# Two-layer kernel: the decay scans of the second layer write into the tile they read, and that tile gets two buffers

## The chip, the cores and the metric

One NeuronCore of a Trainium2 chip runs the whole program. The metric is device time in microseconds (us) of one launch. The engines are TensorE (PE; its weight loads are listed as PEld), VectorE (DVE), ScalarE (ACT), GpSimd (POOL) and SyncE (SP), which issues nearly all DMAs.

## The reference

The input is `x` of shape (16, 512, 128): 16 batches of 512 tokens. Two layers follow each other.

```python
xn = _layernorm(x)
x  = x + L0_attn(xn) + L0_ffn(xn)      # selective-scan mixer; 8 experts, top 1
xn = _layernorm(x)
x  = x + L1_attn(xn) + L1_ffn(xn)      # the layer that this change is in
```

The second layer's mixer is a causal linear attention with 16 heads, a decay for each head and token, and a factor `lam_ts` that is picked by the "level" of the pair of tokens (how high the highest bit is in which their positions differ):

```python
g  = A * softplus(x @ Wdt.T + dt_bias)         # per token and head
cg = cumsum(g, axis=1)
decay = exp(cg[t] - cg[s]) for s <= t, else 0
Wmat  = scores * decay * lam_ts                # scores = Q K^T / 8
Y = einsum('bhts,bshd->bthd', Wmat, V)
out = layernorm(Y @ Wout.T + x) * ln_g + ln_b
```

The second layer's other branch is a small gated recurrence over the 16 batches with a projection at its end.

## The kernel before, in words

**Two phases.** The loop `for i in range(-2, NB + 3)` runs layer one, a batch (a *block*) of 512 tokens at a time, in overlapping stages. The loop `for b in range(NB + 1)` runs the mixer of layer two over the same 16 blocks. In the profiled execution layer one takes the first 300 us and layer two the rest, some 31 us a block. Results of layer one go through HBM (`d_xf`, `d_xh`, `d_xl`, `d_xt`, `d_x1`).

**Second layer, block b.** The 512 tokens are split into chunks of `C` = 32.
- `load1(b)` and `gates(b)` load the block and make the projections (`pp`) and the step sizes; `g3` is the log decay, split into three bf16 parts.
- `factors(b)` turns `g3` into chunk decays (`pe`, then `ex`), makes the level factors `la`, and transposes the level and decay rows (`pld`). Through HBM (`dde`) the decay rows are spread over partitions into the tile **`dd`** by four DMAs (L1102 to L1104); the level rows go through `dld` into `R`.
- `products(b)`: 16 heads, three 512-wide matmuls each into a bank `pT`, copied by ACT into `th_all`.
- `states(b)`: chunk states `pG` into `Gs`, with the tiles `bv`, `t`, `tiles`.
- `diagonal(b)`: four scans on DVE make the decays inside a chunk: each reads a quarter of `dd` and writes a quarter of the tile **`dec`** (L1212 to L1218). Then four multiplications by the level factors, out of the banks `pl`.
- `diagonal2(b)`: four multiplications of `dec` by the scores, out of the banks `pS`; then 64 small matmuls (128 recorded) read `dec` into the bank `pyd`, which is added to `ysum`.
- `upper(b)`, `upper2(b)`: the part between chunks (`pU`, `yq`, `pY`, `aY`), added to `ysum` on POOL, for the last block on DVE.
- `finish(b)`: `pyt` (transpose of `ysum`), `yT`, the output projection `po1` (shown as `b_po`), the sum `o` with the block, layer norm (`lc_st`, `lc_mv`, `lc_r`, `lc_nb`, four activations on `o`, a multiplication on POOL, an addition on DVE) and the store.

**Buffers.** `bt(shape, dtype, tag, name)` takes a tile from a pool by tag. A tag has one buffer unless `BUFS` says otherwise (L503). `dec` and `dd` have one each, 8 KB in a partition. So the scans of block b+1 wait until the 128 `pyd` matmuls of block b have read `dec`, and the DMAs that fill `dd` for block b+1 wait until the scans of block b have read it.

**Lending.** Layer one borrows the second layer's tiles (`lend`, L594 to L622): the split input `xnh`/`xnl` of its projections lies in the buffer of `dec`, the scratch tiles `th`, `xt`, `bx` in the buffer of `dd`.

**Who sets the order.** Every instruction is first recorded by the class `Plan`; `flush()` then simulates all engines with assumed durations and picks, engine by engine, the order in which the instructions are emitted. Each engine then runs its list in that order, and an instruction that waits holds all behind it on the same engine. A sort key takes an operation's due time, the length of what depends on it, a weight by the engine and the name of the written tile, and a small pseudo-random term with a fixed seed:

```python
kind = o.eng[0] + ":" + kind.tensor.name.rstrip("0123456789_")
o.key -= 1000.0 * (URGENT.get(kind, 0.0) + STAGES.get(stage(...), {}).get(kind, 0.0))
o.key += rng.uniform(-JIT, JIT)
```

`URGENT` (L50) has the entry `"v:lent_dec_xnh": -0.5`, for DVE instructions that write the lent tile of that name. All recorded instructions are emitted from one line, L479, so the profile's groups are told apart by tile names.

Of the kernel before, what the change touches and what calls it, by code (L numbers as in the profile page):

```python
# [12 lines left out]
F32 = mybir.dt.float32  # L13
F32R = mybir.dt.float32r
# [9 lines left out]
P = 128  # L24
NG = 4
NH = 16
EPS = 1e-5
C = 32
# [464 lines left out]
def two_layer_kernel(ctx: ExitStack, tc: tile.TileContext, a: dict, out: bass.AP):  # L493
# [6 lines left out]
    sp = ctx.enter_context(tc.tile_pool(name="s", bufs=1))  # L500
    ps = ctx.enter_context(tc.tile_pool(name="ps", bufs=1, space=PSUM))
    dram = ctx.enter_context(tc.tile_pool(name="dram", bufs=1, space=DRAM))
    BUFS = {k: 2 for k in ("xf", "xh", "xl", "vz", "aY", "bv", "vbd")}  # L503
    BUFS.update({"xt": 3, "hh": 3})

    PA, PB = 5000.0, 5000.0

    def bank(name, tag="tr", shape=(P, 512), dt=F32):
        return nc.bank(ps, shape, dt, tag, name)

    def bt(shape, dt, tag, name, bufs=None):
        return nc.tile(sp, shape, dt, tag, name, bufs or BUFS.get(tag, 1))

# [80 lines left out]
    def lend(tag, k, dt, users, cols=T):  # L594
        t = bt([P, k, cols], dt, tag, "lent_" + tag + "_" + (users[0] if users else "w"))
        for i, u in enumerate(users):
            ring.setdefault(u, []).append(t[:, i, :])
        return t
# [4 lines left out]
    wbig = lend("vbd", 4, F32R, []).rearrange("p (s k) c -> p s (k c)", s=2)  # L603
    wbig = wbig[:, 0, :], wbig[:, 1, :]
    lend("vbd", 4, F32, ["x1", "x1", "xn1", "hs"])
    lend("dec", 4, F32R, ["xnh", "xnh", "xnl", "xnl"])


    Gs = wt([P, NH, 17, 8], F32, "Gs")
# [83 lines left out]
    for e in range(8):  # L693
        j = e % 4
# [271 lines left out]
    vbd = []  # L966

    def namer1(b):
        return lambda s: f"b_{s}_{b}"
# [237 lines left out]
    def diagonal(b):  # L1207

        n, d = namer1(b), B[b]
        R = d["R"]  # L1210

        dec = bt([P, NH, NG, C], F32, "dec", n("dec"))  # L1212
        for q in range(4):
            hs = slice(4 * q, 4 * q + 4)
            nc.vector.tensor_tensor_scan(
                dec[:, hs].rearrange("p h j t -> p (h j t)"), d["dd"][:, hs].rearrange("p h t -> p (h t)"),
                upat.rearrange("p q t -> p (q t)"), 0.0, op0=ALU.mult, op1=ALU.add,
            )  # L1218
        Rt = R.rearrange("r h (t j) -> r t h j", j=NG)
        for q in range(4):  # L1220
            pl = bank(n(f"pl{q}"))
            for i in range(8):
                t = 8 * q + i
                nc.tensor.matmul(
                    pl[:, i * 64 : (i + 1) * 64], sell[:, t, :], Rt[:, t], start=True, stop=True
                )
            dv = dec[:, :, :, 8 * q : 8 * q + 8].rearrange("p h j t -> p j h t")
            nc.vector.tensor_tensor(
                dv, dv, pl.rearrange("p (t h j) -> p j h t", h=NH, j=NG), op=ALU.mult
            )  # L1230
        d["dec"] = dec
# [62 lines left out]
    for i in range(-2, NB + 3):  # L1294
# [49 lines left out]
        if i == NB + 1:  # L1344
            states(0)
            diagonal(0)
            products(0, "pj", range(8, NH))
# [15 lines left out]
    for b in range(NB + 1):  # L1363
        nc.base = (NB + 4) * PA + (b + 1) * PB
        nc.start_group(LNEXP)
        if 0 < b < NB:
            states(b)
        if b + 2 < NB:
            load1(b + 2)
        if b + 1 < NB:  # L1370
            gates(b + 1)
        if b:
            finish(b - 1)
        if b < NB:
            if b:
                diagonal(b)
            for q in range(4):
                if b:
                    products(b, heads=range(4 * q, 4 * q + 4))
                if q:  # L1380
                    upper(b, q - 1)
        if b + 1 < NB:
            factors(b + 1)
        if b < NB:
            upper(b, 3)
            upper2(b)
            diagonal2(b)
        if b + 1 < NB:
            nc.start_group(EXPTANH)
            cell_out(b + 1)  # L1390
# [113 lines left out]
```

## Time and profile before

| | |
|---|---|
| median of 3 runs | 829.51 us (827.62 to 831.28) |
| the profiled execution's own time | 828.71 us |
| its span, first to last instruction | 826.5 us |
| busy, share of the span | PE 96%, DVE 89%, ACT 76%, POOL 25% |
| `dec` and `dd`: instructions of layer two | 64 scans, 128 multiplications, 64 DMAs into `dd` |

The span is 2.2 us shorter than the execution's own time; that difference lies around the instructions. Matmuls are pipelined and their ends are modelled, so a PE that is busy all the time is not one at its peak. What idle PE time there is, and what ended it, is read from the list of waits and from the timeline.

### The profile page before, as it was taken

What the parts mean: (1) busy time and instruction counts of PE and PEld (TensorE: products, weight loads), DVE (VectorE), ACT (ScalarE), POOL (GpSimd) and SP (SyncE); (2) the same over time, 40 slices, a digit from 0 to 9 for tenths busy, and PEclk for the clock granted to TensorE, in tenths of its full rate; (3) what the DMA queues carried; (4) which work ended last, traced back from release to release, by engine and by line L of the source; (5) the groups of instructions that cost most, each with busy time, mean ns of one, the idle gap of its engine ahead of it and who ended that gap; (6) DMA issues with size and microseconds to landing.
All of it is one profiled execution on the core that took longest, in us unless ns stands there. A gap on an engine that the chain in (4) does not pass through costs nothing.

```text
span 826.5 us, 27744 instructions
## 1 busy us (share of the span) xinstructions
PE 790.8 (96%) x11432; PEld 605.4 (73%) x11432; DVE 735.5 (89%) x1889; ACT 631.9 (76%) x1322; POOL 206.7 (25%) x236
## 2 busy tenths in 40 slices
PE   7899999999999998999999999999999999999994
PEld 4577878777888776787677778768677778677772
DVE  5799999999998996798989999888999989899885
ACT  6788898989898887876696697587588577587573
POOL 2200000000000110333343343533433523433521
PEclk9799999999999998999999999999999999999998
DMA  9516444334333334254345346435346426536311
GB/s 226 132 52 205 141 154 127 103 113 136 112 109 108 109 115 139 78 135 117 104 128 147 96 130 150 130 94 151 100 123 158 136 79 156 130 87 157 88 52 40
DMA packets 92402, 100.18 MB, mean 121 GB/s; under 512 B 26532, under 2 KB 63788, under 8 KB 90156
## 3 DMA queue, kind: packets, MB, share of 16 engines
q1 hardware_dynamic: 92276, 98.41, 42.5%
q8 instruction: 90, 1.47, 0.7%
q14 instruction: 36, 0.29, 0.1%
HBM read 63.70 MB, written 34.67 MB: 119 GB/s over the span
## 4 chain that ended last, share of the span: by engine, by line
PE 56%; DVE 18%; ACT 15%; DMA 4%; issue 3%; POOL 3%; SPq 0%; ACTq 0%; DVEq 0%; POOLq 0%
PE b_pT L479 11%; PE pg L479 6%; DVE b_dec L479 5%; ACT th_all L479 5%; PE b_pU L479 5%; PE po L479 5%; PE pm L479 4%; PE b_pY L479 3%; PE b_pS L479 2%; DVE b_la L479 2%; PE pC L479 2%; ACT L479 2%; PE pxi L479 2%; PE pz L479 2%; PE b_pp L479 2%
## 5 line engine op out<-in xcount | busy, mean ns | idle before, releaser
L479 ACT COPY th_all<-b_pT 128x512 f32<-128x512 f32 x256 | 145.0, 622 | 25.9 <-PE b_pT L479 20.0
L479 PE MATMUL b_pT<-b_xh,A_h 128*128 128x512 f32 x256 | 108.1, 422 | 1.2 <-DVE b_tiles L479 0.9
L479 POOL TENSOR_TENSOR b_u<-b_u,b_vz 128x704 f32<-128x704 f32 x16 | 27.9, 1743 | 298.7 <-DVE b_vz L479 256.9
L479 PE MATMUL b_pT<-b_xh,A_l 128*128 128x512 f32 x256 | 100.8, 394 | 0.0
L479 PE MATMUL b_pT<-b_xl,A_h 128*128 128x512 f32 x256 | 100.4, 392 | 0.0
L479 ACT ACT_TABLE_LOAD x71 | 91.1, 1283 | 1.9 <-PEq L1494 0.7
L479 DVE TENSOR_TENSOR_SCAN b_dec<-b_dd,upat 128x512 f32<-128x512 f32 x64 | 77.8, 1226 | 4.5 <-PE b_pyd L479 3.0
L479 PEld LDWEIGHTS b_pU<-th_all,Gs 128*32 128x32 f32 x4096 | 61.3, 110 | 19.2 <-issue 9.0
L479 PE MATMUL b_pU<-th_all,Gs 128*32 128x64 f32 x4096 | 70.9, 220 | 2.1 <-ACT th_all L479 0.9
L479 PE MATMUL b_pS<-th_all,b_xf 128*32 128x512 f32 x512 | 60.3, 594 | 0.4 <-ACT th_all L479 0.4
L479 PEld LDWEIGHTS b_pT<-b_xh,A_h 128*128 128x128 f32 x256 | 48.1, 188 | 15.3 <-PE b_pT L479 1.3
L479 PEld LDWEIGHTS b_pT<-b_xh,A_l 128*128 128x128 f32 x256 | 48.1, 188 | 10.9
L479 PEld LDWEIGHTS b_pT<-b_xl,A_h 128*128 128x128 f32 x256 | 48.3, 189 | 6.9
L479 ACT COPY b_yq<-b_pU 128x512 f32<-128x512 f32 x64 | 38.5, 614 | 13.8 <-PE b_pU L479 13.4
L479 DVE TENSOR_TENSOR b_dec<-b_dec,b_pl 128x512 f32<-128x512 f32 x64 | 40.3, 680 | 9.4 <-PE b_pl L479 9.4
L479 DVE TENSOR_TENSOR b_dec<-b_pS,b_dec 128x512 f32<-128x512 f32 x64 | 43.6, 681 | 1.2 <-PE b_pS L479 1.0
L479 DVE TENSOR_TENSOR b_la<-b_ex,b_sp 64x32 f32<-64x32 f32 (+3 forms) x160 | 41.4, 284 | 1.7
L479 ACT ACTIVATE lent_vbd_x<-lent_vbd_x,lb_nb,lb_r 128x128 f32<-128x128 f32 x64 | 29.6, 489 | 11.8 <-DVE lb_nb L479 8.7
L479 DVE TENSOR_TENSOR b_aY<-b_pY,b_la 128x384 f32<-128x384 f32 (+1 forms) x64 | 33.9, 543 | 4.4 <-POOL b_ysum L479 3.0
L479 PE MATMUL pg<-lent_yq_x1h,lent_hh_w 128*128 128x512 f32 x96 | 33.8, 431 | 1.1 <-DVE lent_yq_x1h L479 1.1
L479 PE MATMUL pm<-Gs,ww 128*128 128x512 f32 x64 | 34.5, 621 | 0.0
L479 ACT ACTIVATE b_o<-b_o,b_lc_nb,b_lc_r 128x128 f32<-128x128 f32 x64 | 33.7, 552 | 0.9 <-DVE b_lc_nb L479 0.9
(268 smaller groups left out, 2154.7 us busy)
## 6 DMA issues: line engine op xcount, KB each, us to landing
b_dd<-b_dde SPq DMA_DIRECT2D x64, 256.0 KB, 5.7
b_dld<-b_ld SPq DMA_DIRECT2D x48, 96.0 KB, 2.8
b_R<-b_dld SPq DMA_DIRECT2D x16, 288.0 KB
d_x<-lent_vbd_x SPq DMA_DIRECT2D x16, 256.0 KB, 3.4
d_xt<-lent_vbd_x SPq DMA_DIRECT2D x16, 256.0 KB, 3.7
b_xt<-d_xt SPq DMA_DIRECT2D x16, 256.0 KB, 3.7
d_xf<-th_all SPq DMA_DIRECT2D x16, 256.0 KB, 2.0
d_xh<-lent_yq_x1h SPq DMA_DIRECT2D x16, 256.0 KB, 3.6
```

Of the source, the lines that this page charges most:

```text
L479: o.inst = getattr(getattr(self.nc, o.eng), o.name)(*o.args, **o.kw)
```

## The change

The scans of block b write over `dd` itself, and everything that read or wrote `dec` afterwards goes on that tile (`dec` is now a view of it). The tag `dec` is gone and `dd` has two buffers, so the memory is the same. Layer one's `xnh`/`xnl` are lent one buffer of `dd`, and its `th`, `xt`, `bx` the other. The DMAs for block b+1 now wait for the last reader of block b-1 (`pyd`), and the scans of block b+1 wait for their DMA alone.

```diff
-    BUFS = {k: 2 for k in ("xf", "xh", "xl", "vz", "aY", "bv", "vbd")}
+    BUFS = {k: 2 for k in ("xf", "xh", "xl", "vz", "aY", "bv", "vbd", "dd")}
...
-    lend("dec", 4, F32R, ["xnh", "xnh", "xnl", "xnl"])
+    lend("dd", 4, F32R, ["xnh", "xnh", "xnl", "xnl"])
...
-        dec = bt([P, NH, NG, C], F32, "dec", n("dec"))
+        dec = d["dd"].rearrange("p h (j t) -> p h j t", j=NG)
         for q in range(4):
             hs = slice(4 * q, 4 * q + 4)
             nc.vector.tensor_tensor_scan(
-                dec[:, hs].rearrange("p h j t -> p (h j t)"), d["dd"][:, hs].rearrange("p h t -> p (h t)"),
+                d["dd"][:, hs].rearrange("p h t -> p (h t)"), d["dd"][:, hs].rearrange("p h t -> p (h t)"),
                 upat.rearrange("p q t -> p (q t)"), 0.0, op0=ALU.mult, op1=ALU.add,
             )
```

No instruction is added or removed. The lent tile that was `lent_dec_xnh` is now named `lent_dd_xnh`, and what was `b_dec` is `b_dd`; the entry `"v:lent_dec_xnh"` of `URGENT` no longer matches a tile.

## The prediction

> **What bounds the kernel now.** I read the page first, then PE's own waits, the instructions on `dec`, the stretches of the second layer and the timeline of the last block, and last the two instruction orders, engine by engine.
>
> ```profile
> PE 790.8 (96%) x11432; PEld 605.4 (73%) x11432; DVE 735.5 (89%) x1889; ACT 631.9 (76%) x1322; POOL 206.7 (25%) x236
> ...
> L479 DVE TENSOR_TENSOR_SCAN b_dec<-b_dd,upat 128x512 f32<-128x512 f32 x64 | 77.8, 1226 | 4.5 <-PE b_pyd L479 3.0
> ```
>
> PE is the bound. The scans cost DVE 77.8 us, and DVE stood idle ahead of them for 4.5 us: 3.0 us until `pyd` had read `dec`, and 1.3 us for a DMA into `dd`, by the answer on the tile. These are the two waits that the change loosens. What reaches PE is in PE's own waits:
>
> ```profile
> PE b_pe L479 <- DVE b_g L479: 4.4, 6, 1.6
> ...
> PE b_pyd L479 <- DVE b_dec L479: 0.9, 1, 0.9
> ```
>
> The columns are us in total, times, longest. PE waited for `dec` once, 0.9 us, and that at 812 us, in the last block. Its largest DVE wait is for the log decays `g3` (shown as `b_g`) ahead of `pe`. In 18 stretches of 25 us from 350 to 800 us, PE is busy 439.2 of 450 us: 10.8 us idle in all. That is the most that a better order of the middle can give back; `pyd` returns every 29.9 us (605.54, 635.59, 665.44) at best and every 30.9 us on average (389.26 to 759.88, 12 blocks), which says the same: some 12 us.
>
> The end is different:
>
> ```profile
> 800.00:825.00 25.00, 14.24 (x412) 9.87 (x404) 15.92 (x45) 9.03 (x21) 3.82 (x3) 0.87 0.17 47
> ```
>
> After the start of the slice the columns are PE, PEld, DVE, ACT, POOL, the granted clock and the DMAs. Here no engine is full: a chain through all of them sets the end, and each step on it costs its own time.
>
> **The change part by part.** Counts stay: 64 scans at 1226 ns, 128 multiplications at 680 ns, 64 DMAs. A scan that writes where it reads is not in this trace; the nearest rows are the multiplications, which already write over `b_dec`, at 680 and 681 ns, like other two-input operations of their size (684 ns for the split of `xnh`). I take 1226 ns unchanged; the reach is -0.1 to +0.1 us a scan, no more than 6 us on DVE and nearly none on PE in the middle.
>
> `dd`'s DMAs now wait for `pyd` of two blocks before instead of the last block's scans. Both are past when the DMAs issue at a block's end, so nothing behind them on SP's queue is held longer: 0. Layer one's orders of PE, DVE and ACT are the same until its last block, so the lost weight `"v:lent_dec_xnh"` moves nothing there; on SP two constant loads near 18 us, `sell` and `upat`, swap, and `upat` is wanted first at 314 us: 0.
>
> What remains is the order of layer two, which `Plan` makes anew. Three things in it have a price.
>
> *The middle, DVE.* The scans now stand ahead of `pyd`. Before, `pyd` of the last block mostly stood behind the products of head 6; now it stands behind head 8 to head 15, and `ysum`, `pyt`, `po1` and the layer norm follow it into the second half of the block. The waits of 3.0 and 1.3 us go. They were on DVE and PE waited for `dec` only at the end, so I count 0 on PE; the bounds are 0 and -4.3 us. The first DVE wait to come after them is the 9.4 us for `pl`, which PE itself sets.
>
> The Trainium skill (Trainium Kernel Development and Optimization, Best Practices) advises two buffers so that DMA overlaps compute. By that rule the second `dd` buffer would be a gain; the trace shows the load hidden but for 1.3 us.
>
> *The middle, PE.* In blocks 9, 10 and 13 the new order is `pyd`, two `pl` banks, then `pyt`, which needs `ysum`. From the end of `pyd` to `pyt` takes 0.96 us (813.38 to 814.34 in the last block: 0.22 us, the 0.68 us addition, 0.06 us); two `pl` banks fill 0.41 us. So 0.55 us of new PE wait, three times: +1.7 us. Against it, changes between whole-array products and products on a part of it fall from 219 to 214, at some 0.1 us each (a `pT` matmul follows another after 0.23 us, but after 0.31 to 0.34 us on either side of `pyd`): -0.5 us.
>
> *The end.* In the old order `po1` of block 13 and `pyd` of block 14 stood ahead of head 3 of the last block's products; in the new one they come after head 15, between the third and the fourth `pl`. So the layer norms of blocks 13 and 14, which ran beside the last products, now fall into the tail. I count from the first `pl` of block 15 (796.70 us), which comes 1.09 + 1.31 = 2.4 us earlier since those two are gone from ahead of it:
> - PE: three `pl` 0.8, `po1` 1.1, `pyd` 1.3, `pl` 0.4, first `pS` 0.9: at 4.5 us.
> - DVE: multiplication, `Gs`, `ysum` of block 14 and the norm statistics of block 13 among them, 2.7 us with latency: at 7.4 us.
> - ACT: latency and two `lc_r` 0.7, table load 1.28, `hh` 0.5, four activations on `o` 1.65, table load 1.28, four `yq` with `yT` between at 0.5 each: at 15.4 us. Before, the products' copies covered these.
> - PE: last `pY` 0.6, `po1` of block 14 1.1, last `pS` 0.9: at 18.0 us.
> - DVE: other work to 18.6, the last multiplication 0.6, then five `ysum` 1.0, `aY3` 0.6, the statistics of block 14 1.2: at 22.0 us.
> - ACT: `lc_r` 0.6, load 1.28, four activations 1.65, `yT` of block 15 0.5: at 26.1 us. `po1` of block 15 1.2, and DVE's last `o` starts at 27.4 us.
>
> Before, that `o` started at 816.86 us, 20.2 us from the same mark. So +27.4 - 20.2 - 2.4 = +4.8 us. These lines show the old tail, where the four activations were over 4.7 us before `yT` wanted ACT:
>
> ```profile
> 807.31 1.28 ACT L479 ACT_TABLE_LOAD   x1
> 808.61 1.65 ACT L479 ACTIVATE b_o<-b_o,b_lc_nb,b_lc_r 128x128 f32<-128x128 f32 x4
> 815.03 0.58 ACT L479 COPY b_yT<-b_pyt 128x512 f32<-128x512 f32 x1 [4.77 <-PE b_pyt L479]
> ```
>
> After the load of 1.28 us the next activation starts within 0.02 us, so I price a load at 1.28. The Trainium skill (ScalarE: Activation LUTs, What ACT_TABLE_LOAD costs) gives about 1283 ns for the load and about 1380 ns of drain on top. By that rule the three loads of the new tail would add 3 x 1.38 = 4.1 us, an estimate from that page, which speaks further against the change; the trace has no such gap.
>
> The tail's sum is good to about 4 us either way: work that I laid end to end may overlap, or waits that I left out may come.
>
> **Sum.** 4.8 + 1.7 - 0.5 = +6.0 us. On the profiled execution's 828.7 us that is 834.7; on the median, which is 0.8 us higher, 835.5. I say 835. The likeliest case's own range is 831 to 840.
>
> **The rivals.**
> - *Faster.* The free scans let DVE reach `g3` earlier, so that PE's waits of 4.4 us for `g3`, 1.0 us for `pld` and most of the 4.3 us go: -8 us; and the tail overlaps, +2 instead of +4.8. With +1.2 for the rest (1.7 - 0.5) that is 829.5 - 4.8 = 824.7; for 822 the middle must give nearly all its 10.8 us. For it: the waits exist and DVE is 89% busy. Against it: in the new order the `g3` chain still lies between the multiplications by `pS`. It decides if the tail costs under 2 us.
> - *No difference.* The tail costs 4.8 us and the middle gives back as much: 829 to 832. For it: the middle is planned anew in every block, with 10.8 us of waits to draw from. Against it: nothing in the new order takes the `g3` wait away.
> - *Worse in the middle.* With the layer norms pushed to where DVE multiplies by `pl` and `pS`, the `g3` chain comes later and PE waits another 0.7 us in each of 13 blocks: 835 + 9 = 844. For it: in blocks 5 and 12 statistics of the norm stand among those multiplications. It decides if the waits of `pe` for `g3` pass 10 us.
> - *It doesn't do what it says.* If an in-place scan were slower than 1226 ns, by more than 0.3 us each, DVE would gain 1.2 us a block and pass PE: above 844.
>
> **How the numbers follow.** The measurement tells about 0.5%, 4.15 us, from no change: 825.4 and 833.7 are the limits. My forecast's case has 0.50, worse in the middle 0.20, a slow in-place scan 0.02, no difference 0.15, faster 0.13. Of the forecast's case about a twelfth, 0.04, ends under 833.7 and belongs to "same". So faster 0.13, same 0.19, slower 0.68. The range reaches down to 826 (which leaves out about 0.13) and up to 845 (about 0.07 above).
>
> **What would show it.** Right: the first `pl` of block 15 comes earlier against the end of the span, the tail from there grows from 29.8 us to 34 to 39 us; the four activations on `o` of block 14 stand between the last statistics and the last `yT`; DVE's waits for `pyd` at the scans are gone, 1226 ns stays; PE waits for `ysum` ahead of `pyt` near 0.55 us in blocks 9, 10 and 13. Wrong: a tail of about 30 us; `g3` waits far from 4.4 us; scans of another length; a start of layer two that moves.

## The result, and the profile after

The changed kernel takes 842.26 us (median of 4 runs, 841.59 to 844.64), the kernel before in the same comparison 829.50 us. The ratio is 1.0159 [1.0129, 1.0189]: 12.8 us slower. The profiled execution took 842.17 us, its span 840.4 us, 13.9 us more than before.

First the page, with the engines' busy time and the group of the scans:

```profile
span 840.4 us, 27755 instructions
...
PE 794.6 (95%) x11432; PEld 610.2 (73%) x11432; DVE 729.9 (87%) x1889; ACT 633.7 (75%) x1322; POOL 206.5 (25%) x236
...
L479 DVE TENSOR_TENSOR_SCAN b_dd<-b_dd,upat 128x512 f32<-128x512 f32 x64 | 75.5, 1209 | 1.5 <-DMA b_dd<-b_dde 1.3
```

The change does on DVE what it says: an in-place scan takes 1209 ns instead of 1226, and the idle time ahead of the scans falls from 4.5 to 1.5 us, with no wait for `pyd` left. No count changed. PE is busy 3.8 us longer and the span is 13.9 us longer, so some 10 us of the loss are PE time in which nothing ran.

The mark of the prediction, the first `pl` of block 15, splits it. Here is the mark before, and then, of the kernel after, the first and the last instructions of PE's timeline behind it, and DVE's last sum `o`:

```profile
796.70 0.88 PE L479 MATMUL b_pl<-b_R,sell 72*128 72x64 bf16 x24
```

```profile
802.40 0.88 PE L479 MATMUL b_pl<-b_R,sell 72*128 72x64 bf16 x24
803.12 1.14 PE L479 MATMUL b_po<-pkl,b_yT 128*128 128x128 f32 x8
804.19 1.30 PE L479 MATMUL b_pyd<-b_vbd,b_dd 128*32 128x32 f32 x128
...
828.97 2.08 PE L479 MATMUL b_po<-pkl,b_yT 128*128 128x128 f32 x8 [1.91 <-ACT b_yT L479]
```

```profile
831.08 0.69 DVE L479 TENSOR_TENSOR b_o<-b_po,b_xt 128x512 f32<-128x512 f32 x1 [0.56 <-PE b_po L479]
```

| | before | after | difference | with the 2.4 us of `po1` and `pyd` that moved past the mark |
|---|---|---|---|---|
| span's start to the mark | 796.70 | 802.40 | +5.7 | **+8.1** (forecast +1.2) |
| mark to the span's end | 29.8 | 38.0 | +8.2 | **+5.8** (forecast +4.8) |

The tail came nearly as forecast. The stretch ahead of it did not. PE's own waits of the after kernel from 350 to 800 us (us in total, times, longest) show what stands there now:

```profile
PE b_pY L479 <- ACT b_yq L479: 2.6, 1, 2.6
PE b_pU L479 <- DVE Gs L479: 2.3, 4, 0.8
PE b_pU L479 <- issue: 1.9, 2, 1.4
PE b_pe L479 <- DVE b_g L479: 1.8, 4, 0.8
PE b_pl L479 <- issue: 1.8, 1, 1.8
PE b_pyt L479 <- POOL b_o L479: 1.7, 1, 1.7
```

The wait for `g3` ahead of `pe`, the largest before, fell from 4.4 to 1.8 us. In its place PE waits for `yq`, for `Gs`, and in two groups for nothing that the profile names ("issue"). The 1.7 us that the profile puts down to POOL (`b_o`) is doubtful: it falls inside a group of four `pyt` matmuls, two of which had already run, so it is more likely of the "issue" kind too. By the 25 us windows PE's idle time from 350 to 800 us went from 10.8 to 16.0 us, +5.2. Two stretches at half clock come on top, behind the two longest waits. This is the window around the first, before and after:

```profile
500.00:525.00 25.00, 25.00 (x518) 20.08 (x512) 22.85 (x57) 20.50 (x41) 11.92 (x14) 1.00 0.56 141
```

```profile
500.00:525.00 25.00, 21.57 (x348) 17.58 (x352) 18.49 (x45) 20.14 (x39) 8.87 (x13) 0.93 0.44 115
```

The columns are PE, PEld, DVE, ACT, POOL, the granted clock, the DMAs. A mean clock of 0.93 over 25 us is 3.4 us at half clock, by estimate a loss of 1.7 us; 620 to 630 us, at 0.83, gives the same. So 5.2 + 2 x 1.7 = 8.6 us, near the 8.1 of the table.

ACT's timeline of that place, block 5, shows who was late:

```profile
499.59 0.30 ACT L479 ACTIVATE b_lc_r<-b_lc_mv,eps_c 128x4 f32<-128x4 f32 x1 [3.30 <-DVE b_lc_mv L479]
499.92 0.21 ACT L479 ACTIVATE b_lc_r<-b_lc_r 128x4 f32<-128x4 f32 x1
500.36 1.26 ACT L479 ACTIVATE b_o<-b_o,b_lc_nb,b_lc_r 128x128 f32<-128x128 f32 x3 [0.23 <-DVE b_lc_nb L479]
501.53 0.52 ACT L479 ACTIVATE b_ex<-b_pe 128x448 f32<-128x448 f32 x1
501.95 0.56 ACT L479 CAST b_ld<-b_pld 96x512 bf16<-96x512 f32 x1
502.54 1.28 ACT L479 ACT_TABLE_LOAD   x1
503.83 0.58 ACT L479 COPY b_ldr<-b_pld 16x512 f32<-16x512 f32 x1
504.43 0.59 ACT L479 COPY b_yq<-b_pU 128x512 f32<-128x512 f32 x1
```

ACT stood 3.30 us for the statistics of the *previous* block's layer norm. It then did the norm's activations and a table load, and only then the copy of `yq` for which PE had been waiting 2.61 us. In the kernel before, the same copy of `yq` comes ahead of that norm:

```profile
500.19 0.58 ACT L479 COPY b_yq<-b_pU 128x512 f32<-128x512 f32 x1 [0.77 <-PE b_pU L479]
...
504.00 0.30 ACT L479 ACTIVATE b_lc_r<-b_lc_mv,eps_c 128x4 f32<-128x4 f32 x1 [0.81 <-DVE b_lc_mv L479]
```

This is not so in every block. From block 1 to block 14 the new order has the previous block's norm ahead of the last `yq` in blocks 5 and 11 only, and in block 11 only its first 0.3 us; the old order has it in none. In the other blocks the norm follows the four `yq` in both orders.

### The profile page after: what moved, and what is told of

It reads as the page before. It is cut to its first block, busy times and chain, and to the rows that moved or that the text cites. A ratio compares the mean times of both kernels' runs of the same rounds, so it can differ in the third digit from the quotient of the medians.

```text
span 840.4 us, 27755 instructions
## 1 busy us (share of the span) xinstructions
PE 794.6 (95%) x11432; PEld 610.2 (73%) x11432; DVE 729.9 (87%) x1889; ACT 633.7 (75%) x1322; POOL 206.5 (25%) x236
## 4 chain that ended last, share of the span: by engine, by line
PE 52%; DVE 23%; ACT 13%; DMA 5%; issue 4%; POOL 2%; SPq 1%; DVEq 0%; ACTq 0%; POOLq 0%
PE b_pT L479 9%; PE pg L479 7%; DVE b_dd L479 6%; PE po L479 5%; PE b_pU L479 4%; PE b_pS L479 4%; ACT th_all L479 4%; PE pm L479 3%; PE b_pY L479 3%; ACT L479 2%; PE pC L479 2%; DVE Gs L479 2%; PE pxi L479 2%; PE b_pG L479 2%; PE pz L479 2%
## 5 line engine op out<-in xcount | busy, mean ns | idle before, releaser
L479 DVE TENSOR_TENSOR_SCAN b_dd<-b_dd,upat 128x512 f32<-128x512 f32 x64 | 75.5, 1209 | 1.5 <-DMA b_dd<-b_dde 1.3
L479 PE MATMUL b_pS<-th_all,b_xf 128*32 128x512 f32 x512 | 63.4, 609 | 0.6 <-issue 0.6
L479 DVE TENSOR_TENSOR b_dd<-b_dd,b_pl 128x512 f32<-128x512 f32 x64 | 41.1, 679 | 7.7 <-PE b_pl L479 7.6
L479 DVE TENSOR_TENSOR b_dd<-b_pS,b_dd 128x512 f32<-128x512 f32 x64 | 43.0, 679 | 2.9 <-PE b_pS L479 2.8
L479 DVE TENSOR_TENSOR b_la<-b_ex,b_sp 64x32 f32<-64x32 f32 (+3 forms) x160 | 37.8, 263 | 1.6
L479 ACT ACTIVATE lent_vbd_x<-lent_vbd_x,lb_nb,lb_r 128x128 f32<-128x128 f32 x64 | 29.7, 490 | 11.7 <-DVE lb_nb L479 8.6
L479 PE MATMUL b_pY<-pk,b_yq 128*128 128x128 f32 x256 | 34.9, 277 | 3.0 <-ACT b_yq L479 2.6
L479 POOL TENSOR_TENSOR b_x<-b_x,b_hh 128x512 f32<-128x512 f32 x16 | 20.8, 1303 | 58.9 <-DMA b_x<-d_x 39.4
L479 PEld LDWEIGHTS b_pY<-pk,b_yq 128*128 128x128 f32 x256 | 28.5, 140 | 8.4 <-ACT b_yq L479 4.1
```

The costliest lines, as they stand in the source:

```text
L479: o.inst = getattr(getattr(self.nc, o.eng), o.name)(*o.args, **o.kw)
```

## The experiments

Every run is compared with the kernel before on the same chip: 828.58, 830.21, 829.25 and 828.51 us in the four groups. "To the mark" and "tail" are as in the table above. In some kernels the order is a list written into the program; their instructions carry other line numbers, but are the same instructions.

### Is it the order, or the tile and its buffers?

The first run puts the changed buffers under the old order. The next two take one order up to the first `pT0` of block 14 and the other from there.

```diff
     # Plan.flush(), ahead of emission
+    order = [ops[i] for i in ORDER]   # the list that the kernel before emits
```

> The changed kernel (in-place scans, two buffers of dd), but every engine's instructions in the order of the kernel before. Order theory (all of the 12.8 us comes from the new order, none from the buffers or the in-place scan): 829.5 us, within 2 us, and the 3.0 us that DVE waited for pyd ahead of the scans may go without a gain on PE. Buffer theory (the in-place scan, or where the tiles now lie, slows instructions): 836 us or more, with longer scans or multiplications.

Measured: 827.82 us, ratio 0.9991 [0.9968, 1.0014]. To the mark 797.82, tail 29.8 us. The group of the scans:

```profile
L720 DVE TENSOR_TENSOR_SCAN b_dd<-b_dd,upat 128x512 f32<-128x512 f32 x64 | 77.7, 1224 | 1.0 <-DMA b_dd<-b_dde 1.0
```

The waits of DVE are gone here too, and PE gains nothing from it: those 3.5 us were never on its path. The tile, the second buffer, the in-place scan and the loan cost nothing. As far as the interval tells, all of the loss is in the order.

```diff
+    order = ...   # in words: old order to the first pT0 of block 14, new order from there
```

> The changed kernel's buffers; the old order up to the first product of block 14 in the second layer, the new order from there. Tail theory (the new order of the last two blocks costs 38.0 - 29.8 - 2.4 = 5.8 us by itself): 835 us. Rival (the tail is only long because the middle left it out of step): 831 us or less.

Measured: 833.22 us, 1.0071 [1.0044, 1.0097]; tail 37.7 us.

```diff
+    order = ...   # in words: new order to the first pT0 of block 14, old order from there
```

> The changed kernel's buffers; the new order up to the first product of block 14, the old order from there. If middle and tail add up: 842.3 - 5.8 = 836.5 us. If the tail costs nothing by itself: 842 us.

Measured: 838.91 us, 1.0133 [1.011, 1.0157]; tail 30.0 us. So the new tail alone costs 833.22 - 828.58 = 4.6 us and the new middle alone 838.91 - 828.58 = 10.3 us. Their sum, 14.9 us, is somewhat over the 12.8 us of the whole change. The second run was expected at 836.5 us and came 2.4 us above that.

### Why did the plan make another order?

The emitted lists show the difference in one number: after which head of block b's products the `pyd` of block b-1 stands. Before, it is head 5 to 8 in the middle, and head 2 in the last block. After, it is head 9 to 15 from block 3 on, and 15 in the last. My theory: the scans of block b waited for `pyd` of block b-1, so all of block b depended on `pyd`, and that length is in its sort key. Without the dependency only `ysum`, `pyt`, `po1` and the layer norm depend on it, and these are urgent only at the very end. This kernel gives the dependency back to the plan, and only to the plan; the buffers stay as changed.

```diff
-            nc.vector.tensor_tensor_scan(
+            i = nc.vector.tensor_tensor_scan(
                 ...
+            if b:
+                nc.ops[i].deps.add(B[b - 1]["pyd"])
...
-                nc.tensor.matmul(
+                d["pyd"] = nc.tensor.matmul(
```

> The changed kernel; only in the plan the scans of block b are still told to depend on the last pyd matmul of block b-1 (no wait on the chip comes with it). The plan's key counts what follows an operation; without that dependency pyd is followed only by ysum and the layer norm, and is sent behind the products of heads 9 to 15; with it, pyd stands behind heads 5 to 9 again. Lost urgency theory: 829 us, 826 to 832. Rival (any newly drawn order loses against the old one, wherever pyd stands): 836 us or more, since this order too is another one on PE from the start of the second layer.

Measured: 833.60 us, 1.0037 [1.0022, 1.0053]; to the mark 802.14, tail 29.7 us. `pyd` stands behind head 5 to 9 again, and behind head 2 in the last block. Of 12.8 us, 842.26 - 833.60 = 8.7 come back (the two kernels before differ by 0.7), the whole of the tail with them. The time is 1.6 us above the theory's range and 2.4 us under the rival's, so most of the loss, but not all of it, goes with the lost dependency. ACT's timeline shows the tail as it was, with the norm's activations 4.47 us ahead of need:

```profile
814.07 1.65 ACT L479 ACTIVATE b_o<-b_o,b_lc_nb,b_lc_r 128x128 f32<-128x128 f32 x4
820.19 0.58 ACT L479 COPY b_yT<-b_pyt 128x512 f32<-128x512 f32 x1 [4.47 <-PE b_pyt L479]
```

The mark itself comes back by only 0.3 us, from 802.40 to 802.14, although 2.4 us of work stand ahead of it again; 3.3 us of its lateness against before lie ahead of the first `pG` of block 1 (356.12 before, 359.39 here).

What is left, 3.4 us against before, is no more than what another draw of the plan's random term does:

```diff
-JIT, SEED = 50.0, 3
+JIT, SEED = 50.0, 1
```

> The kernel before with another seed of the plan's random term: pyd stays behind heads 5 to 9. Lost urgency theory: within 4 us of 829. Rival (the old order is a lucky draw): 835 us or more.

Measured: the kernel before with seed 1 takes 835.47 us, 1.0068 [1.0045, 1.0091]. That is outside the 4 us of the theory and at the rival's limit: the old order is in part a lucky draw, by some 5 us.

> The changed kernel with another seed: pyd stands behind heads 10 to 15 in nearly every block, and block 14's pyd behind head 15 of block 15. Lost urgency theory: 838 to 848 us, with a tail of some 38 us from the first pl of block 15. Rival (this draw was unlucky): 829 to 834 us.

Measured: 853.34 us, 1.0269 [1.024, 1.0299]; to the mark 814.0, tail 37.4 us.

> As the run with seed 1, another seed again: 838 to 848 us by the lost urgency theory, 829 to 834 us if the draw alone decides.

Measured: seed 2 gives 846.33 us, 1.0192 [1.0169, 1.0215]; tail 36.3 us. So with the dependency in the plan three orders took 829 to 835 us, without it three took 842 to 853 us. The ranges don't meet, and with seed 1 on both sides the change costs 853.34 - 835.47 = 17.9 us: the loss isn't one unlucky draw. The two new draws took more than the theory's 848 us in one case (853.34) and lay in its range in the other. But the draw alone moves the time by 6 us in the one kind and 11 us in the other.

### What in the new middle costs the time?

**`pyd` early.** If the place of `pyd` cost the time, putting it back should return it. This kernel keeps the new order but for the `pyd` of eleven blocks.

```diff
+    for b in range(3, 14):      # in the finished order
+        # take out the pyd of block b-1, and put it behind pT6 of block b
+        order[at + 1 : at + 1] = mine
```

> The changed kernel in its own order, but in blocks 3 to 13 the pyd matmuls stand again behind the products of head 6 instead of next to the other short matmuls (pU, pl). Instruction supply theory (runs of short matmuls use up PE's instructions faster than they are fetched): PE's waits with no releaser in the middle fall from 4.2 us to under 1 us, the half clock after 620 us goes, about 837 us. Rival (the waits on ACT and POOL of the layer norms make the middle slow): 841 to 843 us, with waits of PE on ACT and POOL as before.

Measured: 843.08 us, 1.0179 [1.0149, 1.0209]. The theory missed. The waits without a releaser in the middle fell from 4.3 to 1.1 us and no half clock was left from 360 to 800 us, yet the time stayed. The waits of PE from 350 to 800 us say where it went:

```profile
PE b_pY L486 <- ACT b_yq L486: 4.4, 2, 2.6
PE b_pe L486 <- DVE b_g L486: 4.0, 7, 1.3
```

**A weight instead of a move.** The plan itself is asked for an early `pyd`, and the rest is planned around it.

```diff
-    "t:b_pp": 0.5, "t:b_pyt": -1.0, ...
+    "t:b_pp": 0.5, "t:b_pyd": 8.0, "t:b_pyt": -1.0, ...
```

> The changed kernel with the weight 8 for pyd in the plan's key: pyd stands behind the products of heads 0 to 3 of its block, ysum still behind all scans, block 14's pyd still behind head 15 of block 15. If the place of pyd is what matters: middle as before, tail as changed, 835 us. If ysum and what follows it matter: 838 us or more.

Measured: 843.79 us, 1.0203 [1.0148, 1.0257]; to the mark 804.59, tail 37.7 us. `pyd` now stands behind heads 0 to 3 of the products, but `ysum` still stands behind the scans on DVE, and the norm behind that. In neither of these two runs does an earlier `pyd` alone bring anything; by the lists, what it feeds stays late.

```diff
     "t:b_pyd": 8.0, as above
+    order = ...   # in words: this order to the first pT0 of block 14, the order of before from there
```

> The same order up to the first product of block 14, the old order from there. If middle and tail add up: 5.4 us less than the run before. A version that beats both kernels would be under 826 us; I expect 829 to 834.

Measured: 843.91 us, 1.0186 [1.0147, 1.0225]; to the mark 811.93, tail 30.6 us. The tail is 7 us shorter and the stretch ahead of it 7 us longer. I had expected the two to add up. Of these 7 us, 2.4 are `po1` and `pyd`, which stand ahead of the mark again, and 2.4 lie ahead of the first `pG` of block 1 (353.87 and 356.31). The other 2.5 weren't traced to a cause.

**Without the norm.** If the late layer norm costs the time, a kernel without it should lose little by the new order. Both kernels leave out the norm's statistics and activations of layer two.

```diff
+    order = [o for o in order if not norm(o)]   # norm: writes b_lc_*, or an activation on b_o
```

> The changed kernel's buffers in the old order, with the second layer's layer norm left out (its statistics, the rstd pair, the shift and the four activations on o). Serves as the base for the next run: first pl of block 15 at 790 to 797 us after the start of the span, total 818 to 829 us.

Measured in the old order: 823.93 us, 0.9939 [0.9919, 0.9958]; tail 26.4 us.

> The same in the new order. Late norm theory (the layer norms, pushed into the second half of a block, hold up the copies of yq on ACT and the multiplications on DVE, and that is what the middle lost): the first pl of block 15 comes no more than 1 us later than in the old order without the norm (with the norm: 5.7 us later), the tail's excess of 8.2 us falls to about 3, the total within 4 us of the run without the norm in the old order. Rival (the late pyd and ysum themselves, and the runs of short matmuls): the mark stays 4 us or more later.

Measured in the new order: 830.70 us, 1.002 [0.9994, 1.0047]; tail 32.0 us. The norm costs 829.25 - 823.93 = 5.3 us in the old place and 842.26 - 830.70 = 11.6 us in the new one, so 6.2 us of the change are the norm's. The other half, 830.70 - 823.93 = 6.8 us, comes without it, where I had expected 4 at most. The mark comes 2.5 us later than in the old order without the norm, between the 1 us of the theory and the 4 us of the rival, and the tail's excess is 5.6 us instead of about 3.

The stretch from the first `pG` of block 1 to the mark leaves out the start of layer two. To compare like with like, the new order gets back the 2.4 us of work that moved past the mark:

| | first `pG` of block 1 | mark | stretch | with the 2.4 us |
|---|---|---|---|---|
| old order, with the norm | 356.12 | 796.70 | 440.6 | 440.6 |
| new order, with the norm | 354.68 | 802.40 | 447.7 | 450.1 |
| old order, without | 354.20 | 795.97 | 441.8 | 441.8 |
| new order, without | 356.88 | 798.50 | 441.6 | 444.0 |

With the norm the new order costs 9.5 us in this stretch, without it 2.2. By the two other runs that keep the old order and the norm there, the stretch takes 442.4 us (changed buffers, old order) and 439.7 us (old middle with the new tail, with the 2.4), so 2.2 us is no more than the scatter and 7.3 us is well above it. With the dependency back in the plan, and the norm in place, it takes 442.8 us (802.14 - 359.39). Each figure is from one profiled execution. The wait of 2.6 us for `yq` and the half clock behind it are gone, by estimate 4.3 us of the 7.3; the waits of the "issue" kind stay (1.8 us for `pl`, 1.5 for `pU`), and so does the one put down to POOL (1.8 us). Where the other 3 us come from stays open. Without the norm ACT also has some 27 us less to do and DVE some 20, so these runs show that the loss needs the norm's work, and not which of its places costs what.

```diff
     # in words: without the norm, new order, and the pyd of blocks 2 to 12 moved as in "pyd early"
```

> The changed kernel in its own order without the layer norm of the second layer, and pyd of blocks 3 to 13 behind head 6: both suspected causes taken out. If they are all of the middle's loss: the stretch from the first pG of block 1 to the first pl of block 15 is 439 us or less (441.8 in the old order and 441.6 in the new without the norm, of which the new has 2.4 us of work less ahead of the mark); total 826 to 829 us. Rival (a third cause): 442 us or more, total as without pyd moved, 830.7.

Measured: 830.57 us, 1.0019 [0.9995, 1.0043]; that stretch is 440.8 us, tail 31.7. The stretch lies between the two expectations and the total doesn't move: an early `pyd` brings nothing here either.

**The waits for nothing.** With seed 1 PE's waits without a releaser at `pyd`, `pl` and `pS` are 12.3 us, which would explain much of its 11 us over the change with its own seed. Moving `pyd` away from the other short matmuls should take them away.

```diff
     # in words: seed 1, and the pyd of blocks 2 to 12 moved as in "pyd early"
```

> The changed kernel with seed 1 in the plan, whose run took 853.3 us with 12.3 us of PE waits without a releaser at pyd, pl and pS and five stretches of half clock in the middle; here pyd of blocks 3 to 13 stands behind head 6 again, all else in that order. Instruction supply theory (a run of short matmuls outruns the fetch of PE's instructions, and the long waits that come of it halve the clock): those waits fall under 3 us and most of the half clock goes, 835 to 842 us. Rival (late layer norms make the loss and PE only waits elsewhere): 848 us or more.

PE's waits from 360 to 812 us, first with seed 1 alone:

```profile
PE b_pyd L479 <- issue: 5.5, 2, 2.9
PE b_pl L479 <- issue: 5.0, 2, 2.9
PE b_pS L479 <- issue: 1.8, 2, 1.3
```

and then with `pyd` moved:

```profile
PE b_pyt L486 <- DVE b_ysum L486: 7.5, 3, 4.7
PE b_pe L486 <- DVE b_g L486: 3.9, 6, 1.4
PE b_pY L486 <- ACT b_yq L486: 1.9, 1, 1.9
```

Measured: 856.60 us, 1.0327 [1.0291, 1.0362], no faster than 853.34. The waits without a releaser are down to some 1.5 us, and PE waits for `ysum` and `g3` instead. Taking these waits away gains nothing here either, as the rival had it; that DVE and ACT are late anyway in this order, and that these waits only lie in front of that, is my reading of the list.

## Why the prediction was wrong, and where it was right

**Right: the direction, and the tail step by step.** The forecast was +6 us, the measured change +12.8. From the mark at 802.40 us, forecast and measured:

| step of the tail | forecast | measured |
|---|---|---|
| DVE: last statistics of block 13 | 7.4 | 7.4 |
| ACT: the last `yq` | 15.4 | 15.3 |
| PE: the last `pS` | 18.0 | 17.9 |
| DVE: last statistics of block 14 | 22.0 | 22.5 |
| ACT: `yT` of block 15 | 26.1 | 26.5 |
| DVE: `o` starts | 27.4 | 28.7 |

ACT's timeline shows the four activations of block 14 where the prediction put them, between the last statistics and the last `yT`; before, they had been over 4.7 us ahead of it:

```profile
824.96 0.30 ACT L479 ACTIVATE b_lc_r<-b_lc_mv,eps_c 128x4 f32<-128x4 f32 x1 [7.28 <-DVE b_lc_mv L479]
825.29 0.20 ACT L479 ACTIVATE b_lc_r<-b_lc_r 128x4 f32<-128x4 f32 x1
825.51 1.28 ACT L479 ACT_TABLE_LOAD   x1
826.80 1.65 ACT L479 ACTIVATE b_o<-b_o,b_lc_nb,b_lc_r 128x128 f32<-128x128 f32 x4
828.36 0.56 ACT L479 COPY b_yT<-b_pyt 128x512 f32<-128x512 f32 x1
```

The load takes 1.28 us and the next activation follows within 0.02 us, so the row's price was right. The drain of about 1380 ns that the Trainium skill adds (ScalarE: Activation LUTs, What ACT_TABLE_LOAD costs) isn't seen here either. Of the 1.3 us that the table misses at its end, 0.9 are the last `po1`: 2.08 us instead of 1.16, at half the clock (the window from 825 to 840 us shows 0.50 and PE busy for 3.2 of 15 us).

**Right: the terms set to zero.** In-place scans kept their length; the two DVE waits went and were worth nothing to PE; SP and the loan cost nothing. The first run shows all of it together as 0.9991 [0.9968, 1.0014]. For the lost weight it is the plan itself: with the entry renamed to `"v:lent_dd_xnh"`, every engine's list is the same.

**Wrong: the term for the middle.** The forecast had +1.7 - 0.5 = +1.2 us, the trace shows +8.1 to the mark. The step that failed is *The middle, DVE*: "`ysum`, `pyt`, `po1` and the layer norm follow it into the second half of the block", and then "I count 0 on PE". The move was seen, and priced only by the two DVE waits that it takes away. Those were indeed worth nothing. What the new order puts there was left at 0 without a reason, although the third rival gave the same thing 9 us. In its place the runs show 7.3 of 9.5 us in the stretch that go when the norm is left out. The largest single piece is in block 5: ACT did the previous block's norm ahead of the last `yq`, PE waited 2.61 us for that copy, and 3.4 us at half clock followed, by estimate 1.7 us more. The half clock, twice 1.7 us, had no term in the sum. Nor had the waits of the "issue" kind, 0.6 us before and 4.3 after; but the runs that took such waits away gained no time, so they can't be added to the loss.

The term of 1.7 us for `ysum` ahead of `pyt` was too large as well. The 0.41 us that it gives two `pl` banks is the row of one bank of 8 matmuls; two banks take 0.65 us (x16), which would have left 0.3 us instead of 0.55. Of its three blocks, block 13 shows 0.37 us, block 10 no such wait, and in block 9 a wait of 1.80 us without a releaser, between the first and second `pl` bank, stands there instead.

**The rival that came nearest** was *worse in the middle*, at 844 us, to which I gave 0.20. Its number is near 842.26 partly by luck. The norm is what the runs without it show for most of that stretch, but not the way the rival had it: it was to show in every block, in the waits of `pe` for `g3` passing 10 us, and these fell to 1.8. The norm moved ahead of a `yq` in two blocks, and the late step was ACT's copy of `yq`, not DVE's `g3`. *Faster* failed by the point that it named: its tail had to cost under 2 us.

**What stays open.** How the middle's loss divides among its waits can't be read from runs that move one thing: two moves of `pyd` (its place, and a weight on it) left the time as it was while other waits came up in place of the old ones. The weight on `pyd` leaves no norm ahead of a `yq` in blocks 1 to 14, and that kernel is as slow, so the norm's place on ACT is not the only way to lose the time. Of what the new order costs without any norm (6.8 us by the medians, 8.1 by the two spans), 3.2 us are tail (32.0 - 26.4, less the 2.4 moved past the mark), 2.2 are the stretch, and 2.7 lie ahead of the first `pG` of block 1 (354.2 to 356.9). That last part is likely scatter: in five kernels with the same new order up to there, this `pG` starts between 354.1 and 356.9 us. The new order on the old buffers wasn't tried: its scans of block b stand ahead of the `pyd` that frees `dec`, and the two might wait for each other. None of the kernels beat the one before; the first run equals it.

## What to carry to other kernels

Where a planner's key counts what depends on an operation, a dependency is also a priority: taking one away frees the instruction that waited, and lets go everything that stood in front of it. Price the work that now comes later, by what it stands ahead of on each of its engines, and not only the wait that disappears. If the freed wait isn't on the bound engine's path, keep the old order (here it was worth 12.8 us against nothing gained), or give the planner the dependency without the wait (here that brought back 8.7 of the 12.8 us).

## What the runs showed of the hardware

- **PE stops where the profile names nothing to wait for.** This came behind runs of short matmuls. PE's timeline of block 9 of the changed kernel:

```profile
615.84 1.55 PE L479 MATMUL b_pU<-th_all,Gs 128*32 128x64 f32 x96
617.20 1.30 PE L479 MATMUL b_pyd<-b_vbd,b_dd 128*32 128x32 f32 x128
618.44 0.56 PE L479 MATMUL b_pl<-b_R,sell 72*128 72x64 bf16 x13
620.80 0.26 PE L479 MATMUL b_pl<-b_R,sell 72*128 72x64 bf16 x3 [1.80 <-issue]
```

  237 matmuls go in 3.2 us, and then PE stands 1.80 us inside one group. The trace has a packet of 16,384 bytes on the instruction queue that starts at 618.6 us, 2.2 us before PE goes on. The sixteen kernels of this case have 28 waits of this kind over 1 us behind 340 us; 27 of them end 2.2 to 2.9 us after such a packet starts, one 3.9 us after, while the packets come some 5.9 us apart. The Trainium skill (Runtime: NRT & Kernel Launch, Instruction fetch mechanics) has instructions fetched in blocks of 16 KiB and calls the cost of crossing one mostly hidden. If these waits are that cost, it was not hidden here, up to 2.9 us at a time (seed 1). Moving `pyd` away from the other short matmuls took most of them away (4.3 to 1.1 us), so the order has a part in them. That the packet is the cause was not tested by itself.
- **Half the clock behind waits under 3 us, but not behind every one.** The half clock of 3.4 us followed waits of 2.61 and 1.80 us, while in the kernel with `pyd` early a wait of the same 2.61 us left the clock full. In the old order without the norm, 3.4 us of half clock followed two waits of 0.91 and 0.81 us within 2 us of each other. The Trainium skill (TensorE: Matmul & The Clock Gate, Why this matters for your kernels) warns of gaps above some 3 us; these were shorter. The same page (What's actually happening) has a free-running window of 3413 ns, which would fit the 3.4 us and the difference between two like waits; no run here tests that.
